# The opening of a fused triangle-and-gate kernel: first shift ahead of the second power, held-back centres, statistics whose lead grows over 33 steps

## The chip, the cores and the metric

The kernel runs on one core of one Trainium2 chip. The metric is device time in microseconds (us) of one execution. A core has five engines that run their own instruction streams in order and meet only at semaphores: TensorE (PE; its weight loads are shown as PEld), VectorE (DVE), ScalarE (ACT), GpSimd (POOL), and SyncE (SP), which here issues nearly all DMA transfers.

## The reference

Two layers on a 384 x 384 x 128 array, in float32. Only the first half of layer 0 is touched by the change:

```
z     = layernorm(x)                                 # over 128 channels
left  = (z @ Wl + bl) * sigmoid(z @ Wlg + blg)
right = (z @ Wr + br) * sigmoid(z @ Wrg + brg)
core  = einsum('bikh,bjkh->bijh', left, right)
x     = x + sigmoid(x @ Wg + bg) * (layernorm(core) @ Wout + bout)
```

Layer 1 is a gated row operation: `left * sum(right) * gate`, a projection, a residual and a layer norm. In this data the norm weights are one and the biases zero, but the kernel does not rely on it.

## The kernel before

The kernel has three stages. Stage 1 (up to about 1032 us) computes `left` and `right` and stores them to DRAM as `lr_d`. Stage 2 does the einsum, one channel at a time. Stage 3 does the output projection and all of layer 1. Every instruction is recorded with `seq`, so each engine executes its instructions exactly in the order in which the code issues them.

**Chunks, steps, halves.** Stage 1 works on 144 chunks of 8 rows of 128 tokens. A chunk is two *steps* of 4 rows, a step is two *halves* of 2 rows; 288 steps in all. For a half, `back` issues two matmuls of a 128 x 128 column tile with the 128 x 512 weights `wz` (L367; each leaves two records in the trace), two sigmoids on ACT (L377, tile `sg`, five buffers), and two products on DVE (L379, into `lr`). The PSUM tile `pr` has three buffers.

**Layer norm.** The norm's scale is applied after the matmul: `rs` is the scale of the sigmoid (L377) and a scalar of the product (L379). The mean is taken off before it. The work on a chunk's statistics runs ahead of its matmuls:

- `stats` (L264): one DVE instruction a row, from the row load `xt` (five buffers) into `st`. For the first eight chunks (PLAIN) the rows lie in the large tile `stage`.
- `powers` (L276 to L280): five small DVE operations for a *batch* of chunks, giving the variance in `nd` and parts of the mean in `mv`. `mv` has one buffer, `nd` two (for chunks from 8 on).
- `power` (L287): the power -0.5 on POOL, 8 columns at a time, into `rs`. A batch whose last power is issued joins the list `means`.
- `centres` (L297, L298, and L300 for the first eight chunks): small DVE operations that turn `nd` into the mean, with `rs` as an input.
- `store_nd` (L342 to L345), for chunks from 8 on: PE transposes `nd`, ACT copies it to `ndt` (one buffer), SP stores it to DRAM as `nd_d`. It is called at the end of step 2b - 9 for a batch that begins with chunk b (2b - 7 for chunks 8 to 11).
- `load_shift` (L140): SP loads a row of `nd_d` into `bc`, six steps before its step.
- `shift` (L312, or L315 and L316): POOL takes the mean off. For the first eight chunks it works on the rows in `stage`, which PE then transposes and ACT copies (`front`, L327 and L328). From chunk 8 on it works on the columns `xc`, loaded already transposed (L135).

**Order in a step of the main loop** (k counts steps): first up to two powers while k is at most 40, then one; then POOL's shifts, two steps ahead; then for each half `back`, after the first half `centres` and the next step's `front`, then possibly `powers` of a waiting batch, then `stats`; at the end of the step `store_nd`, the loads of columns, shift rows and row chunks, and one slice of 1 MB of finished `lr` (L353). At step 4, four shifts are done ahead, and then POOL loads another code library (L447, the code exchange), which the broadcast of L315 needs; no POOL work goes on meanwhile. At the end of step 20 `late_weights` (L228 to L235) prepares weights of the later stages on DVE, with `m2` as its own tile; at the end of step 21 PE uses `m2` in `late_products` (L241).

**The lead.** At step k the statistics run up to step k + min(25, 7 + k): two steps of statistics are done in each step until k = 18, then one. Batches are of 1 chunk for chunks 0 to 9, of 2 for chunks 10 to 17, then of 4. `powers` of a waiting batch are issued once its statistics are done and both `means` and `pows` are empty. Row chunk n (11 to 25) is asked for at step n - 7 and needs the buffer of chunk n - 5.

Of the kernel before, what the change touches and what calls it, by code (L numbers as in the profile page):

```python
# [8 lines left out]
F32 = mybir.dt.float32  # L9
# [5 lines left out]
P = 128  # L15
# [4 lines left out]
def triangle_then_gated_row_kernel(ctx: ExitStack, tc: tile.TileContext, a: dict, out: bass.AP):  # L20
# [15 lines left out]
    NG8, C = x_nat.shape[1], x_tok.shape[2]  # L36
# [6 lines left out]
    XR = 8  # L43
# [12 lines left out]
    def seq(ins):  # L56

        return tc.keep_in_program_order(ins)
# [4 lines left out]
    def load(dst, src, queue=nc.sync):  # L63
        seq(queue.dma_start(out=dst, in_=src))
# [12 lines left out]
    chunks = [(kb, ig, c) for kb in range(NB) for ig in range(NG) for c in range(G // XR)]  # L77
    kept = {(NB - 1, ig): None for ig in range(NG - KEEP, NG)}
    end2 = ctx.enter_context(ExitStack())
    with ExitStack() as ctx2:  # L80
# [16 lines left out]
        with tc.tile_pool(name="p1w", bufs=5, side="right") as wp, \  # L97
# [7 lines left out]
            NQ = XR // 4  # L105
            AHEAD, LEAD = 6, 25
# [2 lines left out]
            loaded, normed = {}, {}  # L109
            lr, full = {}, []  # L110
            batches, at = [(n, n + 1) for n in range(PLAIN)], PLAIN
            for size in [1, 1, 2, 2, 2, 2] + [4] * len(chunks):
                if at < len(chunks):
                    batches.append((at, min(at + size, len(chunks))))
                    at = batches[-1][1]
            batch = {n: b for b in batches for n in range(*b)}
            terms, pows = {}, []
# [105 lines left out]
            def late_weights():  # L223

                m2 = wp.tile([P, C], F32, tag="m2", name="m2", bufs=1)
                seq(nc.vector.tensor_scalar(m2, avg, go, -0.5, ALU.mult, ALU.mult))  # L228

                seq(nc.vector.tensor_add(wleft, wleft, weq))
                seq(nc.vector.tensor_add(bleft, bleft, beq))

                seq(nc.vector.tensor_scalar(lns, lns, -1.0, None, ALU.mult))  # L235
                return m2
# [29 lines left out]
            def powers(own, lo, hi):  # L266

                if lo == 0:
                    g = XR * (own[1] - own[0])
                    terms[own] += [sp.tile(s, F32, tag=t, name=t, bufs=c)[:, :g] for t, s, c in  # L270
                                   (("mv", [P, 4 * XR, 2], 1),
                                    ("nd", [P, 4 * XR], 2) if own[0] >= PLAIN else ("nd0", [P, XR], PLAIN),
                                    ("rs", [P, 4 * XR], 7) if own[0] >= PLAIN else ("rs0", [P, XR], PLAIN))]
                st, mv, sd, rs = (t[:, lo:hi] for t in terms[own])
                dv = st[:, :, 1]
                seq(nc.vector.tensor_add(mv, st[:, :, 1:3], st[:, :, 4:6]))  # L276
                seq(nc.vector.tensor_sub(dv, dv, st[:, :, 4]))
                seq(nc.vector.tensor_scalar(sd, mv[:, :, 1], 4.0 / C, 4.0 * EPS, ALU.mult, ALU.add))
                seq(nc.vector.tensor_mul(dv, dv, dv))
                seq(nc.vector.tensor_add(sd, sd, dv))  # L280
                pows.extend((own, c, min(c + XR, hi), (lo, hi)) for c in range(lo, hi, XR))

            def power():

                own, lo, hi, span = pows.pop(0)
                sd, rs = (t[:, lo:hi] for t in terms[own][2:])
                seq(nc.gpsimd.tensor_tensor(rs, sd, mhalf[:, :hi - lo], ALU.pow))  # L287
                if hi == span[1]:
                    means.append((own, span))
# [11 lines left out]
                    centred.add(own)  # L301

            centred = set()
            means = []

            def shift(n, q, rows=slice(0, 4)):
# [23 lines left out]
            def first_step():  # L330

                pairs = slice(0, 2), slice(2, 4)
                for s in pairs:
                    shift(0, 0, s)
                for s in pairs:
                    front(0, 0, s)

            def store_nd(own):

                g = XR * (own[1] - own[0])  # L340
                pt = tps.tile([P, 4, P], F32, tag="pt", name="pt")
                seq(nc.tensor.transpose(pt[:g, 0], nds.pop(own), ident))  # L342
                ndt = dp.tile([4 * XR, P], F32, tag="ndt", name="ndt", bufs=1)
                seq(nc.scalar.activation(ndt[:g], pt[:g, 0], AF.Copy, scale=0.5))  # L344
                seq(nc.sync.dma_start(  # L345
                    out=nd_d[own[0]:own[1]].rearrange("n (i k) -> (n i) k", k=P), in_=ndt[:g]
                ))
# [50 lines left out]
            given = 0  # L398

            def stats_to(count):  # L400

                nonlocal given
                while given < min(count, len(halves2)):
                    n, q, half = halves2[given]
                    stats(n, q, half)
                    given += 1
                    if half == 1 and q == NQ - 1:
                        ready.append(n)

            ready = []  # L410
            for k in range(AHEAD):
                for half in range(2):
                    stats_to(given + 1)
                    if k > 0 and half == 0:
                        centres(len(means))
                    if k == 1:
                        weights(half)
                if k == 0:
                    fold()
                    powers((0, 1), 0, 4)  # L420
                    power()
                elif k == 1:
                    powers((0, 1), 4, XR)
                    power()
                elif k < AHEAD - 1 and k % NQ == 1:
                    powers(batch[k // NQ], 0, XR)
                    power()
                if k == 1:
                    first_step()
                if k == 2:  # L430
                    shift(*steps[1])
            shifted = 2
# [2 lines left out]
            waiting = batches[AHEAD // NQ:]  # L435
            for k, (n, q) in enumerate(steps):
                early = len(means)
                for _ in range(min(len(pows), 1 if k > 40 else 2)):
                    power()
                early = early if k > 40 else len(means)  # L440
                more = 4 if k in (4, len(steps) - 6) else 1
                while shifted < min(len(steps), k + 2 + more):
                    shift(*steps[shifted])
                    shifted += 1
                if more > 1:
                    lib = library_config.all_libraries[10] if k == 4 else library_config.standard
                    seq(nc.gpsimd.load_library(lib))  # L447
                turned = [b for b in batches[PLAIN:] if NQ * b[0] - (TURN if b[0] >= PLAIN + 4 else TURN - 2) == k]
                for half in range(2):
                    if k == 0:  # L450

                        back(n, q, half, (lambda: front(*steps[1])) if half else None)
                    else:
                        back(n, q, half)
                        if half == 0:
                            centres(early)
                        if half == 0 and k + 1 < len(steps):
                            front(*steps[k + 1])
                    if half == 0 and not means and not pows and waiting and 2 * NQ * waiting[0][1] <= given:
                        own = waiting.pop(0)  # L460
                        powers(own, 0, XR * (own[1] - own[0]))
                    stats_to(2 * (k + min(LEAD, AHEAD + k + 1)) + half + 1)
                if q == NQ - 1:
                    del loaded[n], normed[n], columns[n]
                for b in turned:
                    assert b in centred, (k, b, waiting[:1], pows, means)
                    store_nd(b)
                if q == NQ - 1:
                    load_columns(n + 4)
                for m, mq in steps[k + FETCH:k + FETCH + 1]:  # L470
                    if m >= PLAIN:
                        load_shift(m, mq)
                for m in fetch.get(k, []):
                    load_chunk(m)
                store_slice()
                if k == 4:
                    for t, src in later:
                        load(t, src)
                if k == 20:
                    m2 = late_weights()  # L480
                if k == 21:
                    late_products(m2)
                if k == len(steps) - 2 * G // 4 + 16:
                    assert not full
                    for h in range(2):
                        load_h(h)
# [134 lines left out]
    with ExitStack() as ctx3:  # L621
# [5 lines left out]
        wp, sp, op, up = pool("p3w", 4), pool("p3s", 4), pool("p3out", 3), pool("p3u", 18)  # L627
# [215 lines left out]
        f, fetched = 0, 4 * RG  # L843
# [107 lines left out]
```

## Time and profile before

| | us |
|---|---|
| median of three runs | 3178.45 (3176.88 to 3178.5) |
| the profiled execution | 3176.98 |
| its span, first to last instruction | 3175.2 |
| first matmul of stage 2 (L580) | 1032.43 |
| PE busy over the span | 3144.1 (99%) |

PE is the engine that sets the time. In a row of an engine's timeline the columns are: start, time taken by the group, engine, line, operation, output<-inputs, shape, count, and in brackets the idle time of the engine before it with what ended it. In a row of the table of stretches the columns are: the stretch, its length, then busy time (and instructions) of PE, PEld, DVE, ACT and POOL, then the granted PE clock (1.00 is full), the busy share of the DMA engines, and GB/s. In the list of waits they are: who waited, for whom, us in all, times, the longest. A wait is put down to the link that came last, which need not be its cause.

### The profile page before, as it was taken

Reading aid. Unit: us, or ns where it says so; the run is one execution under the profiler, and the core shown is the slowest. Engines: PE = TensorE matmul, PEld = TensorE weight load, DVE = VectorE, ACT = ScalarE, POOL = GpSimd, SP = SyncE. Lnnn points to the kernel's source line nnn. Section 1 sums busy time; section 2 is a strip of 40 time slices with the busy share of each in tenths; the row PEclk is TensorE's granted clock in tenths of the full one; section 3 lists DMA queues with packets and bytes.
Section 4 is the critical chain, followed back from the end, with each engine's and each line's share of the span. In section 5 each row is a group of like instructions: output and inputs, shape, how many; then the busy total and the mean of one; then the engine's idle time right before and its main releaser. Section 6 shows DMA issues by size and latency. Waiting matters only on the chain.

```text
span 3175.2 us, 44349 instructions
## 1 busy us (share of the span) xinstructions
PE 3144.1 (99%) x11344; PEld 1875.8 (59%) x11344; DVE 2452.9 (77%) x7201; ACT 1811.9 (57%) x3793; POOL 2384.1 (75%) x3045
## 2 busy tenths in 40 slices
PE   8999999999999999999999999999999999999998
PEld 3444444444444666666666666677777777777776
DVE  8878888888875555555555788888888888888998
ACT  4444444444444333433433577777777777777776
POOL 5888888888886666666665587787788888888887
PEclk9999999999999999999999999999999999999999
DMA  4787878878782999999999865666666666666552
GB/s 157 289 326 271 329 297 308 315 288 337 272 327 86 266 283 281 285 282 282 284 282 282 302 229 211 216 225 222 218 223 218 224 217 223 219 220 219 209 209 110
DMA packets 474829, 797.41 MB, mean 251 GB/s; under 512 B 21329, under 2 KB 385297, under 8 KB 458194
## 3 DMA queue, kind: packets, MB, share of 16 engines
q1 hardware_dynamic: 473280, 792.61, 72.7%
q8 instruction: 94, 1.54, 0.2%
q10 hardware_dynamic: 1234, 1.77, 0.2%
q14 instruction: 157, 1.29, 0.1%
q0 software_dynamic: 64, 0.20, 0.0%
HBM read 508.14 MB, written 286.36 MB: 250 GB/s over the span
## 4 chain that ended last, share of the span: by engine, by line
PE 95%; POOL 2%; DVE 1%; issue 1%; DMA 1%; ACT 1%; SPq 0%; ACTq 0%; POOLq 0%; DVEq 0%
PE pr L367 28%; PE pc L580 23%; PE py L750 8%; PE pr L721 8%; PE pg L738 8%; PE pl L739 8%; PE pg L690 8%; PE py L751 4%; POOL rs L287 1%; DVE lr L379 1%; POOL xc L316 0%; DVE st L264 0%; DMA xt<-in_x_nat_dram 0%; POOL bc L315 0%; DMA stage<-in_x_nat_dram 0%
## 5 line engine op out<-in xcount | busy, mean ns | idle before, releaser
L367 PE MATMUL pr<-wz,xc 128*128 128x512 f32 x2176 | 939.9, 592 | 5.0 <-ACT sg L377 4.3
L377 ACT ACTIVATE sg<-pr,rs 128x256 f32<-128x256 f32 x1152 | 483.2, 470 | 522.3 <-ACT sg L377 346.4
L580 PE MATMUL pc<-rr,lrh 128*128 128x384 f32 x2304 | 743.3, 486 | 0.3 <-DVE lr L379 0.3
L367 PEld LDWEIGHTS pr<-wz,xc 128*128 128x128 f32 x2176 | 409.8, 190 | 522.7 <-issue 433.6
L379 DVE SCALAR_TENSOR_TENSOR lr<-pr,rs,sg 128x256 f32<-128x256 f32 x1152 | 502.3, 478 | 197.5 <-ACT sg L377 197.5
L580 PEld LDWEIGHTS pc<-rr,lrh 128*128 128x128 f32 x2304 | 452.0, 196 | 291.8 <-issue 1.1
L785 ACT ACTIVATE py<-py,nm,rs 128x128 f32<-128x128 f32 x1149 | 491.8, 429 | 158.2 <-DVE u L743 80.1
L750 PEld LDWEIGHTS py<-wo,u 128*128 128x128 f32 x2304 | 376.6, 191 | 97.5
L591 DVE TENSOR_TENSOR csum<-csum,ct 128x1152 f32<-128x1152 f32 x127 | 176.2, 1387 | 333.8 <-ACT ct L589 333.8
L750 PE MATMUL py<-wo,u 128*128 128x128 f32 x2304 | 402.1, 275 | 0.0
L589 ACT COPY ct<-pc 128x1152 f32<-128x1152 f32 x127 | 142.2, 1119 | 445.2 <-PE pc L580 439.7
L712 POOL TENSOR_TENSOR cs<-ct,rt 128x384 f32<-128x384 f32 x380 | 378.8, 998 | 7.6 <-PE pr L721 4.1
L820 POOL TENSOR_TENSOR yt<-yt,lnb 128x384 f32<-128x384 f32 x380 | 379.7, 1001 | 2.9 <-DVE yt L814 2.6
L316 POOL TENSOR_TENSOR xc<-xc,bc 128x512 f32<-128x512 f32 x272 | 345.2, 1269 | 23.9
L287 POOL TENSOR_TENSOR rs<-nd,mhalf 128x8 f32<-128x8 f32 (+1 forms) x145 | 235.7, 1628 | 157.4 <-ACT ndt L344 107.3
L765 DVE BATCH_NORM_STATS2 st<-py 128x6 f32<-128x128 f32 x1152 | 266.4, 287 | 88.9 <-PE py L751 86.9
L561 POOL COPY rr<-lrh 128x768 f32<-128x768 f32 x128 | 193.7, 1513 | 165.3 <-DMA lrh<-lr_d 154.3
L751 PE MATMUL py<-ident,x1T 128*128 128x128 f32 x1152 | 314.0, 273 | 0.0
L721 PE MATMUL pr<-cs,wc 128*128 128x384 f32 x768 | 313.5, 490 | 0.0
L738 PE MATMUL pg<-x1T,mat_L_conv_W_gate 128*128 128x384 f32 x768 | 310.7, 486 | 0.9 <-ACT g L741 0.9
L690 PE MATMUL pg<-xt,mat_L_conv_Wg 128*128 128x384 f32 x768 | 310.7, 487 | 0.3 <-ACT ct L604 0.2
L739 PE MATMUL pl<-x1T,mat_L_conv_W_left 128*128 128x384 f32 x768 | 310.5, 486 | 0.0
(125 smaller groups left out, 4284.6 us busy)
## 6 DMA issues: line engine op xcount, KB each, us to landing
lr_d<-lr SPq DMA_DIRECT2D x128, 1024.0 KB
lrh<-lr_d SPq DMA_DIRECT2D x128, 640.0 KB
xt<-in_x_row_dram SPq DMA_DIRECT2D x96, 768.0 KB
ct<-core_d SPq DMA_DIRECT2D x95, 768.0 KB
rt<-rstd_d SPq DMA_DIRECT2D x95, 768.0 KB
out_dram<-yt SPq DMA_DIRECT2D x94, 768.0 KB
core_d<-ct SPq DMA_DIRECT2D x125, 576.0 KB
xt<-in_x_nat_dram SPq DMA_DIRECT2D x136, 512.0 KB
```

The lines of the kernel that those rows point to most:

```text
L367: seq(nc.tensor.matmul(pr[:, r, :], lhsT=columns[n][:, 4 * q + 2 * half + r, :], rhs=wz, start=True, stop=True))
L377: seq(nc.scalar.activation(sg[r], pr[:, r, 2 * H:], AF.Sigmoid, scale=rs[r]))
L379: seq(nc.vector.scalar_tensor_tensor(t[:, :, c * XR + r0 + r, :], pr[:, r, :2 * H].rearrange("k (h s) -> k h s", s=2), rs[r], sg[r].rearra ...
L580: seq(nc.tensor.matmul(banks[ib], lhsT=t[:, kb, ib * P:(ib + 1) * P, 0], rhs=rr[:, kb], start=(kb == 0), stop=(kb == NB - 1),))
L690: seq(nc.tensor.matmul(pg[:, :N], lhsT=wg0, rhs=r["xT"], start=True, stop=True))
L721: seq(nc.tensor.matmul(pr[:, :N], lhsT=wc, rhs=r["cs"], start=True, stop=True))
L738: seq(nc.tensor.matmul(pg2[:, :N], lhsT=wgate, rhs=r["x1T"], start=True, stop=True))
L739: seq(nc.tensor.matmul(pl[:, :N], lhsT=wleft, rhs=r["x1T"], start=True, stop=True))
L750: seq(nc.tensor.matmul(py[:, s], lhsT=r["u"][:, s], rhs=r["wo"], start=True, stop=False))
L751: seq(nc.tensor.matmul(py[:, s], lhsT=r["x1T"][:, s], rhs=ident, start=False, stop=True, is_transpose=True))
L785: seq(nc.scalar.activation(py[:, s], py[:, s], AF.Identity, bias=bias, scale=scale))
L820: seq(engine.tensor_tensor(yt, yt, lnbb, ALU.add))
```

## The change

1. In the opening, `first_step` (POOL's two subtracts of step 0, PE's transposes, ACT's copies) is issued ahead of the second power rather than after it.
2. In the main loop one power at most is issued in a step. The number of centres to issue is none at steps 5 and 6, the number of batches waiting *before* this step's power at steps after 6, and the number after it at steps up to 4.
3. The lead grows by one a step up to step 11 (to 18), then by one every three steps, and reaches 25 at step 32. Batches of 2 run to chunk 23 (there are seven), and batches of 4 follow from 24 to the end.
4. `mv` has its own tag for each size of batch, with three buffers for one chunk, two for two, one for four. `free` lets the powers of a batch start while fewer batches of its size than that are in flight.
5. `m2` is no longer a tile of its own: it takes the one buffer of `ndt`, which is enlarged to 128 partitions.

The numbers of instructions hardly change: PE has one `nd` transpose more, ACT one copy more, SP one store more. In the order of SP's queue only the stores of `nd` move.

```diff
-            for size in [1, 1, 2, 2, 2, 2] + [4] * len(chunks):
+            for size in [1, 1] + [2] * 7 + [4] * len(chunks):
...
-                m2 = wp.tile([P, C], F32, tag="m2", name="m2", bufs=1)
+                m2 = dp.tile([P, C], F32, tag="ndt", name="m2", bufs=1)
...
-                                   (("mv", [P, 4 * XR, 2], 1),
+                                   ((f"mv{g}", [P, g, 2], {XR: 3, 2 * XR: 2}.get(g, 1)),
...
+            def free(own):
+                flying = {p[0] for p in pows} | {p[0] for p in means}
+                size = own[1] - own[0]
+                return sum(o[1] - o[0] == size for o in flying) < {1: 3, 2: 2}.get(size, 1)
...
-                ndt = dp.tile([4 * XR, P], F32, tag="ndt", name="ndt", bufs=1)
+                ndt = dp.tile([P, P], F32, tag="ndt", name="ndt", bufs=1)
...
                     powers((0, 1), 4, XR)
+                    first_step()
                     power()
                 elif k < AHEAD - 1 and k % NQ == 1:
                     powers(batch[k // NQ], 0, XR)
                     power()
-                if k == 1:
-                    first_step()
...
-                for _ in range(min(len(pows), 1 if k > 40 else 2)):
+                for _ in range(min(len(pows), 1)):
                     power()
-                early = early if k > 40 else len(means)
+                early = 0 if k in (5, 6) else early if k > 6 else len(means)
...
-                    if half == 0 and not means and not pows and waiting and 2 * NQ * waiting[0][1] <= given:
+                    if half == 0 and waiting and 2 * NQ * waiting[0][1] <= given and free(waiting[0]):
...
-                    stats_to(2 * (k + min(LEAD, AHEAD + k + 1)) + half + 1)
+                    stats_to(2 * (k + min(LEAD, AHEAD + min(k + 1, 12 + (k - 11) // 3))) + half + 1)
```

## The prediction

> **What bounds the kernel now.** I read the page first, then a table of engine busy time over stretches of the opening, then what TensorE (PE) waited for, then the timelines of single engines around each wait.
>
> ```profile
> span 3175.2 us, 44349 instructions
> PE 3144.1 (99%) x11344; PEld 1875.8 (59%) x11344; DVE 2452.9 (77%) x7201; ACT 1811.9 (57%) x3793; POOL 2384.1 (75%) x3045
> ```
>
> ```profile
> 0.00:25.00 25.00, 19.14 (x49) 9.17 (x50) 18.33 (x89) 6.78 (x15) 12.73 (x20) 0.93 0.78 281
> 25.00:50.00 25.00, 20.02 (x64) 9.57 (x63) 21.30 (x94) 11.16 (x26) 12.45 (x10) 1.00 0.12 39
> 50.00:75.00 25.00, 23.83 (x72) 10.50 (x70) 24.18 (x94) 13.09 (x32) 14.20 (x11) 1.00 0.46 161
> 75.00:100.00 25.00, 22.57 (x58) 9.59 (x58) 24.28 (x93) 11.40 (x28) 19.66 (x18) 1.00 0.62 215
> 100.00:150.00 50.00, 48.06 (x122) 21.26 (x121) 38.85 (x135) 22.86 (x57) 39.92 (x35) 1.00 0.76 295
> 150.00:200.00 50.00, 48.44 (x115) 21.20 (x114) 37.55 (x124) 23.77 (x59) 36.77 (x34) 1.00 0.85 317
> 200.00:300.00 100.00, 100.00 (x236) 43.85 (x235) 80.96 (x255) 48.82 (x120) 83.47 (x74) 1.00 0.84 324
> ```
>
> The second number of a row is PE's busy time. From 200 us on PE is never idle in this stage, and the change moves nothing in later stages. Before 200 us the idle time is 5.9 + 5.0 + 1.2 + 2.4 + 1.9 + 1.6 = 17.9 us. That is all the change can win, 0.56% of the time, and part of it lies before the first data are there. Losses have no such bound.
>
> ```profile
> PE pr L367 <- ACT sg L377: 10.4, 8, 2.9
> PE pt L327 <- POOL stage L312: 5.3, 4, 3.5
> ```
>
> From PE's timeline, the waits once step 2's tile is there (20.80 us) are 2.07 (at 40.74), 2.91 (47.75), 0.18, 0.30, 0.58, 0.33, 0.58, 0.56, 0.34, 0.63 (the last at 95.21), 0.38 (114.23), 1.56 (143.89) and 1.56 (173.26): 11.98 us. ACT is only the last link: behind it is VectorE (DVE), which executes in order and stands in front of GpSimd (POOL).
>
> ```profile
> 40.74 1.96 PE L367 MATMUL pr<-wz,stage 128*128 128x512 f32 x4 [2.07 <-ACT sg L377]
> 47.75 1.96 PE L367 MATMUL pr<-wz,stage 128*128 128x512 f32 x4 [2.91 <-ACT sg L377]
> ```
> ```profile
> 35.98 0.96 DVE L298 TENSOR_TENSOR nd<-mv,nd 128x8 f32<-128x8 f32 x1
> 44.39 0.17 DVE L297 TENSOR_TENSOR nd<-nd,rs 128x8 f32<-128x8 f32 x1 [2.63 <-POOL rs L287]
> 108.00 0.87 DVE L228 TENSOR_SCALAR m<-avg,col_L_conv_onorm_g 128x128 f32<-128x128 f32 x1
> 141.69 0.65 DVE L297 TENSOR_TENSOR nd<-nd,rs 128x32 f32<-128x32 f32 x1 [2.68 <-POOL rs L287]
> ```
>
> A centre operation (L297, L298) takes 0.17 alone and 0.96 when a GpSimd subtract runs beside it; where its power is not done it waits, and the products `lr` queued behind it wait too.
>
> **The change, part by part.**
>
> *First shift ahead of the second power.* PE's and ACT's order stay. On POOL two half subtracts (0.60 each) go ahead of a power of 1.02. They start when L300 ends (7.38) and end at 8.6; the second power's input comes at 9.24, so that power is not delayed. PE's first transposes come 2.9 us earlier, but PE then waits for step 2's subtract, which waits for DVE and POOL. There the gain is smaller: the centres from 10.37 to 11.54 took 1.17 us beside those subtracts; without them the same three take 0.40 (15.46 to 15.86). So 0.77 us; bounds 0 and 2.9.
>
> *Centres held back.* At steps 5 and 6 none is issued, so DVE no longer meets the 2.63 us wait behind the code exchange (GpSimd idle from 37.9 to 42.67), and PE's 2.91 and 0.18 go. What is late next: six held centre operations at 0.20 come together at step 7, 1.2 us, of which I let 1.1 reach PE (up to 3 if a subtract runs beside them). The wait at 40.74 stays: step 4's centres still stand beside four subtracts. Gain 2.0; bounds 0 and 3.1.
>
> *One power a step, and a slower lead.* Up to step 11 the lead is the same; from 12 to 32 DVE does 5.3 statistics a step for 8, 0.5 us less at 0.195 each, where it was 24.28 of 25 us busy. A subtract follows each power where two powers (3.24) stood before it. The seven waits from 66 to 95 us, 3.3 us, should go; bounds 1 and 3.3. With the count of centres taken ahead of this step's power at every step after 6, DVE no longer stands in front of a power issued in the same step: 0.38 + 1.56 + 1.56 go, 3.5; bounds 2 and 3.5. Sum of gains: 0.8 + 2.0 + 3.3 + 3.5 = 9.6 us.
>
> *m2 in ndt's buffer.* This is the cost that the few words of the change do not show. That pool tag has one buffer. m2 (L228, end of step 20) must wait until the store of batch (14, 15)'s `ndt`, issued at step 19, has left it. That store is on SP's queue behind the load of chunk 25, put there at step 18. This load needs the buffer that chunk 20's statistics free, and with the slower lead the last of those are the statistics of step 20 itself, directly ahead of m2. So DVE stops for a whole round through the queue: one load of 0.5 MB, one `lr_d` store of 1 MB, then the small store. An estimate from the rows: 2.5 us fixed (the first load was issued at 0.73 and used at 3.87, with 0.6 of it transfer) and 1.57 MB at 413 GB/s, 3.8 us: 6.3. Queued behind m2 on DVE are products and statistics; PE needs m2 at L241, which it reached 1.1 us after DVE reached L228 (109.13 against 108.00), and 0.5 pass from m2 to the matmul. Loss 6.3 + 0.5 - 1.1 = 5.7. Bounds: 1 (a small transfer in an empty queue, with part of it covered) and 8 (the 2 KB row issued at 121.04 reached POOL at 127.03, 6.0, and two issues of 1.0 ahead of it).
>
> ```profile
> 121.04 1.69 SPq L140 DMA_DIRECT2D bc<-nd_d  x2
> 127.03 0.79 POOL L315 PARTITION_BROADCAST bc<-bc  x1 [2.27 <-DMA bc<-nd_d]
> ```
>
> ```profile
> 12.60:16.00 3.40, 3.40 (x6) 0.50 1.03 413
> ```
>
> *Half clock.* This row of the table of stretches (PE alone) shows PE's granted clock at 0.50 for 3.4 us soon after PE had stood still for 3.45 us (7.5 to 10.97). There it cost little, for PE waited at 20.80 anyway. A stop of 5.7 us in mid-stage should bring such a stretch with nothing to cover it: 1.6 us; bounds 0 and 1.7. PE's wait for step 2 grows to 1.2 + 2.9 - 0.8 = 3.3 us, nearly as long as that stop; I count half, 0.8 (0 to 1.7). [...]
>
> *Smaller batches, freer powers.* One more `ndt` transpose, 0.1 us. But `nd` keeps two buffers. The powers of (22, 23) come in the first half of step 26 (96 half steps are then given), while (18, 19) leaves its buffer only with the transpose at the end of step 27. DVE stands until PE has done three more halves, and then needs five small operations (0.5), six statistics (1.2) and two products (0.8), plus 0.2 to hand over, before PE goes on: 2.7 us; bounds 0 and 5.2 (three halves of 1.72).
>
> Sum of losses: 5.7 + 1.6 + 0.8 + 2.7 + 0.1 = 10.9 us. Net +1.3. The profiled run took 3176.98 us (span 3175.2 and 1.8 around it), which gives 3178.3; the median of the three runs lies 1.5 higher, which gives 3179.8. I take 3179 between them.
>
> **The rivals.**
>
> *Faster.* The m2 wait does not reach PE (the store is out when DVE arrives, or DVE runs later than I think). It takes 5.7 + 1.6 with it: 3171.7. For it: gains and this loss are of one size, so the sign hangs on it, and in the run before the store was issued 4.6 us ahead of m2 (103.41). Against it: the load in front of the store cannot start before DVE's own last statistics.
>
> *Slower.* SP's queue runs dry of row loads. Chunks 21 to 28 are asked for up to two steps before their buffer is free, and behind them on SP's queue stand the columns and the shift rows. A row is asked for six steps ahead and used by POOL some four steps later, 13.8 us; two steps of wait (6.9) and a queue of 6.0 leave 0.9. From 1 us more a load on, POOL and then PE wait; over eight loads that is 8 us: 3187. Against it: nothing of this kind showed beyond POOL's 2.27 at 127.03, which PE did not feel.
>
> *The DVE-bound waits stay.* If the statistics are not what makes DVE last, most of the 3.3 and half of the 3.5 remain: 3179 + 5 = 3184.
>
> **How the numbers follow.** Net near zero 0.60, faster rival 0.20, slower rival 0.12, waits that stay 0.08. 0.2% is 6.4 us, about what a measurement of this kernel can tell from no change; the bounds are 3172.1 and 3184.8. The likeliest case alone spans 3174 to 3184; taking in the faster rival and most of the slower ones the range is 3171.3 to 3186. Faster 0.20, within 0.62, slower 0.18.
>
> **What would show it.** Right: PE's first transposes near 8.0 us and step 2's near 20.0; no DVE wait for a power between 40 and 50; one PE stop of 5 to 6 us ahead of L241 near 106 us, with L228 waiting for the store of `ndt`, and a row of half clock after it; a PE wait of 2 to 3 us about six steps later, with L278 standing for the `ndt` transpose; no waits like those at 143.89 and 173.26. Wrong: no stop at L241; or POOL waiting for `bc` rows and PE for `xc` between 80 and 150 us; or `lr` still waited for through 66 to 95 us.

## The result, and the profile after

The changed kernel takes 3183.58 us (median of 22 runs, 3180.96 to 3187.39). The kernel before takes 3177.89 on the same chip (22 runs, 3176.55 to 3179.6). The ratio is 1.0018, 95% interval 1.0011 to 1.0025: a loss of 5.7 us that is just inside the 0.2% called "within" in the prediction. The prediction of 3179.0 had the sign, and its range of 3171.3 to 3186 holds the time. The runs also spread more than before: over 6.4 us, where the kernel before spreads over 3.1. Ratios leave out runs that were disturbed; there was one, 5591.69 us in `late_loads` below.

The profiled execution has a span of 3180.1 us, against 3175.2. In the changed kernel the line numbers of stage 1 behind `free` are six higher: L373 is L367 of the kernel before, L350 is L344, L333 is L327, and L322 is L316. The table of stretches of the changed kernel, columns as before:

```profile
0.00:25.00 25.00, 18.64 (x46) 9.13 (x47) 17.43 (x88) 6.86 (x14) 13.61 (x20) 0.93 0.78 279
25.00:50.00 25.00, 22.93 (x72) 11.20 (x71) 23.97 (x101) 12.99 (x30) 13.21 (x10) 1.00 0.16 50
50.00:75.00 25.00, 24.42 (x77) 11.47 (x76) 22.90 (x98) 13.35 (x34) 16.20 (x13) 1.00 0.47 169
75.00:100.00 25.00, 25.00 (x64) 11.02 (x62) 21.20 (x84) 12.48 (x31) 18.76 (x16) 1.00 0.72 241
100.00:150.00 50.00, 37.06 (x88) 17.06 (x87) 31.84 (x118) 16.32 (x40) 30.40 (x27) 0.86 0.68 256
150.00:200.00 50.00, 50.00 (x120) 21.88 (x119) 40.85 (x134) 24.65 (x61) 41.10 (x36) 1.00 0.83 320
```

Everything that the change was to mend is mended: between 25 and 100 us and from 150 us on PE is idle for 2.65 us, where it was idle for 10.1 before. All of that, and more, is lost in the one row from 100 to 150, which has 12.9 us of idle PE and a mean clock of 0.86. On PE's timeline the first row below is step 2's tile, and the four others hold all the stops after it:

```profile
19.73 1.12 PE L333 MATMUL pt<-ident,stage 128*128 128x128 f32 x4 [4.55 <-POOL stage L318]
41.12 1.95 PE L373 MATMUL pr<-wz,stage 128*128 128x512 f32 x4 [2.07 <-ACT sg L383]
53.53 1.95 PE L373 MATMUL pr<-wz,stage 128*128 128x512 f32 x4 [0.56 <-ACT sg L383]
112.15 0.80 PE L241 MATMUL pw<-mat_L_conv_Wout,m 128*128 128x128 f32 x2 [10.21 <-DVE m L228]
140.07 14.01 PE L373 MATMUL pr<-wz,xc 128*128 128x512 f32 x32 [2.72 <-ACT sg L383]
```

The stop ahead of L241 is the wait for `m2`. The timelines of ACT, SP, DVE and POOL in the same kernel show how it comes about:

```profile
95.77 0.25 ACT L350 ACTIVATE ndt<-pt 16x128 f32<-16x128 f32 x1
101.80 0.47 DVE L264 BATCH_NORM_STATS2 st<-xt 128x6 f32<-128x128 f32 x2
102.30 0.34 SPq L128 DMA_DIRECT2D xt<-in_x_nat_dram  x1
102.69 0.42 SPq L359 DMA_DIRECT2D lr_d<-lr  x1
103.21 0.38 SPq L351 DMA_DIRECT2D nd_d<-ndt  x1
110.73 1.37 DVE L228 TENSOR_SCALAR m<-avg,col_L_conv_onorm_g 128x128 f32<-128x128 f32 x1 [8.45 <-DMA xc<-in_x_tok_dram]
110.75 1.26 POOL L322 TENSOR_TENSOR xc<-xc,bc 128x512 f32<-128x512 f32 x1
```

`ndt` is ready at 96.0, but SP, which works in order, issues its store only at 103.21: the load ahead of it waits for the buffer that the statistics at 101.80 free. The store then takes 7.5 us more. DVE waits for it from 102.28 to 110.73. (The row names a load that came last by the profile; the runs below show that it is the store.) L228 then takes 1.37 us, beside a subtract that starts on POOL at 110.75; in the runs below, without such a neighbour, it takes 0.27 to 0.32.

The clock in that stop, in stretches of 2 us of PE alone (columns: stretch, length, PE busy, clock, DMA share, GB/s):

```profile
102.00:104.00 2.00, 0.00 (x0) 1.00 0.94 339
104.00:106.00 2.00, 0.00 (x0) 0.66 0.92 289
106.00:108.00 2.00, 0.00 (x0) 0.50 1.00 416
112.00:114.00 2.00, 1.85 (x9) 0.50 0.11 45
114.00:116.00 2.00, 2.00 (x5) 0.50 0.00 0
116.00:118.00 2.00, 2.00 (x4) 0.50 0.00 0
118.00:120.00 2.00, 2.00 (x6) 0.93 0.02 4
```

The clock falls to half 2.7 us into the stop (104.64, from the share 0.66) and comes back at 118.28, 6.1 us after work has begun again. At full clock those 6.1 us of work would have taken about half as long: the four records of L373 at 41.12 above took 1.95 us at 1.00, and the same four at 43.31 in `m2_in_avg_nd3` (below) took 3.62 at 0.50. So about 3.1 us are lost on top of the 10.21. The stop in the opening is followed by another half-clock stretch, from 19.30 to 22.70, of which 3.0 us are work: 1.5 lost.

**An account of stage 1.** The first matmul of stage 2 comes at 1037.06, for 1032.43 before: 4.63 us later, of the 4.9 us that the spans differ by. The account splits that time in four: the start of step 2's transposes, all of PE's stops after it, half of the time that PE worked at half clock after it (from the clock in stretches of 1 us), and the rest.

| profiled execution | step 2's tile | stops after it | half clock | rest | stage 2 begins |
|---|---|---|---|---|---|
| before | 20.80 | 11.98 | 0 | 999.65 | 1032.43 |
| after | 19.73 | 15.56 | 4.56 | 997.21 | 1037.06 |
| after less before | -1.07 | +3.58 | +4.56 | -2.44 | +4.63 |

The rest is nearly a constant. It is 2.4 lower after, where thirteen stops have become four: by that estimate a stop costs 0.2 to 0.3 more than the idle time shown, which no run tests by itself. The loss of this change is thus not its stops alone, but as much the half clock behind them.

### The profile page after: what moved, and what is told of

It is laid out like the page before. It is cut to its first block, busy times and chain, and to the rows that moved or that the text cites. A ratio compares the mean times of both kernels' runs of the same rounds, so it can differ in the third digit from the quotient of the medians.

```text
span 3180.1 us, 44362 instructions
## 1 busy us (share of the span) xinstructions
PE 3144.7 (99%) x11345; PEld 1878.7 (59%) x11345; DVE 2459.8 (77%) x7208; ACT 1811.9 (57%) x3794; POOL 2402.9 (76%) x3045
## 4 chain that ended last, share of the span: by engine, by line
PE 97%; DVE 2%; DMA 1%; ACT 0%; POOL 0%; issue 0%; SPq 0%; DVEq 0%; POOLq 0%; ACTq 0%
PE pr L373 30%; PE pc L585 23%; PE py L755 8%; PE pr L726 8%; PE pg L743 8%; PE pl L744 8%; PE pg L695 8%; PE py L756 4%; DVE st L264 0%; DVE lr L385 0%; DMA core_d<-ct 0%; DMA xc<-in_x_tok_dram 0%; POOL rs L287 0%; PE pq L703 0%; PE pt L348 0%
## 5 line engine op out<-in xcount | busy, mean ns | idle before, releaser
L373 PE MATMUL pr<-wz,xc 128*128 128x512 f32 x2176 | 940.5, 593 | 2.7 <-ACT sg L383 2.7
L373 PEld LDWEIGHTS pr<-wz,xc 128*128 128x128 f32 x2176 | 411.0, 190 | 519.5 <-issue 432.9
L322 POOL TENSOR_TENSOR xc<-xc,bc 128x512 f32<-128x512 f32 x272 | 345.2, 1269 | 24.0
```

The costliest lines, as they stand in the source:

```text
L373: seq(nc.tensor.matmul(pr[:, r, :], lhsT=columns[n][:, 4 * q + 2 * half + r, :], rhs=wz, start=True, stop=True))
```

## The experiments

Every run is compared with the kernel before on its own chip (medians 3177.0 to 3178.0). "Theory" in the first expectations is the prediction's mechanism with the sizes of the result: the stop for `m2`, and the half clock behind it, make the loss. One execution of each version was profiled, and it is not always a typical one: those of `m2_in_avg_nd3`, `store_on_act` and `nd3_warm` took 1.6 to 2.9 us more than their medians.

### Is it the buffer that m2 shares with ndt?

`m2_in_avg` is the changed kernel with `m2` written over its own input `avg`, which nothing reads later.

```diff
-                m2 = dp.tile([P, C], F32, tag="ndt", name="m2", bufs=1)
+                m2 = avg
```

> The changed kernel, but m2 is written in place over avg, which nothing reads afterwards, so it waits for no store. Theory (m2 waits for ndt's store): the stop of 10.2 us ahead of L241 shrinks to under 1 us and the half clock from 104.6 to 118.3 us goes (6.1 us of work at half speed, 3.1 us): 13 us less than the changed kernel, about 3170, which is 7 to 8 us below the kernel before. The wait of 2.7 us at L278 stays. Rival A (the backlog of loads and lr_d stores would stop the steps there in any case, m2 only meets it first): another wait of 5 us or more appears between 100 and 125 us, on bc or xc, and the time stays above 3177. Rival B (the slower lead is what costs): no gain beyond 2 us.

Measured: 3173.87 us (3172.64 to 3175.47), ratio 0.9987 [0.9978, 0.9996]. Against 1.0018 that is 9.9 us won by this one line. The stop ahead of L241 is down to 0.64. So without the shared buffer the change wins 4 us. It misses the expected 3170: by the account 4.2 us are lost to other half-clock stretches, nearly as much as after (4.56). One follows the next stop of the same profile (PE's timeline, then PE's row in a stretch):

```profile
103.95 0.49 PE L241 MATMUL pw<-mat_L_conv_Wout,avg 128*128 128x128 f32 x2 [0.64 <-DVE avg L228]
129.81 15.97 PE L373 MATMUL pr<-wz,xc 128*128 128x512 f32 x32 [2.88 <-DVE st L264]
```
```profile
131.00:134.00 3.00, 3.00 (x5) 0.50 0.79 251
```

`before_m2_shared` does the reverse: the kernel before, with only the sharing.

```diff
-                m2 = wp.tile([P, C], F32, tag="m2", name="m2", bufs=1)
+                m2 = dp.tile([P, C], F32, tag="ndt", name="m2", bufs=1)
...
-                ndt = dp.tile([4 * XR, P], F32, tag="ndt", name="ndt", bufs=1)
+                ndt = dp.tile([P, P], F32, tag="ndt", name="ndt", bufs=1)
```

> The kernel before with one part of the change alone: m2 takes the buffer of ndt. Theory: the store of ndt was issued at 103.41 there, 4.6 us ahead of m2 at 108.0, since no load held it back; with some 7 us through the queue m2 waits 2 to 4 us and PE 1 to 3, too short for a half clock: 3179 to 3181. If sharing alone carried the whole loss: 3188 or more (a stop of 10 us and half clock after it). If it costs only with the slower lead: 3177.9 unchanged.

Measured: 3182.89 us (3179.53 to 3187.38), ratio 1.0016 [1.0007, 1.0025]. The sharing alone costs 5.0 us, nearly as much as the whole change, and brings the wide spread with it. DVE's and PE's timelines:

```profile
111.50 0.29 DVE L228 TENSOR_SCALAR m<-avg,col_L_conv_onorm_g 128x128 f32<-128x128 f32 x1 [3.07 <-DMA nd_d<-ndt]
```
```profile
111.84 0.49 PE L241 MATMUL pw<-mat_L_conv_Wout,m 128*128 128x128 f32 x2 [2.21 <-DVE m L228]
```

The store is issued at about the same time as after (103.74 for 103.21), and is out at about the same time too (111.5 for 110.7). But DVE comes to L228 at 108.4 here and at 102.3 after, and PE to L241 at 109.6 and at 101.9, so the stop is 2.2 us for 10.2. L241 starts no sooner after (112.15) than here (111.84): what the change wins ahead of that point it gives back in the stop. By the account this profile has two half-clock stretches after step 2 (41.58 to 44.98 and, behind the stop of 2.21 us, 113.26 to 116.66, 3.4 us lost), and its stops, 12.27 us in all, are hardly longer than before's.

### What makes the store late?

`late_loads`: row chunks 21 to 25 are asked for two steps later (26 one step, later ones as before), so that the load of chunk 25 stands behind the store.

```diff
-                fetch.setdefault(max(2 + (n - PLAIN) // 2, n - 7, 2 * n - LEAD - 7), []).append(n)
+                fetch.setdefault(max(2 + (n - PLAIN) // 2, n - (7 if n < 21 else 5), 2 * n - LEAD - 7), []).append(n)
```

> The changed kernel with m2 still in ndt's buffer, but row chunks 21 to 27 are asked for two steps later, when their buffers are free, so the store of ndt does not stand behind a load that waits for the statistics of step 20. Theory: the store goes out when ndt is written, about 97 to 99 us instead of 103.2, and is out when DVE reaches m2 or 1 to 4 us later: PE's stop at L241 under 4 us, no or little half clock, 3170 to 3175. Rival A (a small store needs 7 to 8 us behind stores and loads whatever is ahead of it): stop of 4 to 6 us, 3176 to 3180. Rival C (the order on SP does not matter): 3183 unchanged.

Measured: 3177.11 us, ratio 0.9994 [0.9985, 1.0003], at the edge between the two expectations. Of the 9.9 us that the sharing costs, 6 to 8 are won back: the stop ahead of L241 is 3.23. SP's, DVE's and PE's timelines:

```profile
96.55 0.32 SPq L351 DMA_DIRECT2D nd_d<-ndt  x1
98.81 0.36 SPq L128 DMA_DIRECT2D xt<-in_x_nat_dram  x1
```
```profile
105.32 0.29 DVE L228 TENSOR_SCALAR m<-avg,col_L_conv_onorm_g 128x128 f32<-128x128 f32 x1 [2.54 <-DMA nd_d<-ndt]
```
```profile
105.66 0.80 PE L241 MATMUL pw<-mat_L_conv_Wout,m 128*128 128x128 f32 x2 [3.23 <-DVE m L228]
```

The store is issued as soon as `ndt` is there, 6.7 us earlier than after, and still needs 8.8 us to leave the buffer. The load directly ahead of it explains the late issue, not the slow passage.

`store_on_act` gives the store another queue.

```diff
-                seq(nc.sync.dma_start(
+                seq(nc.scalar.dma_start(
                     out=nd_d[own[0]:own[1]].rearrange("n (i k) -> (n i) k", k=P), in_=ndt[:g]
```

> The changed kernel (3183.6) with m2 still in ndt's buffer, and one line different: the store of ndt is issued on ACT's own queue in place of SP's. Theory A (the store is slow because it stands in SP's queue behind the bytes of loads and slices issued before it, and not because it comes late): on an empty queue it takes some 2.5 us from its issue near 103, VectorE waits until about 106 for 110.7, the stop ahead of L241 falls from 10.2 to about 5 us and with it one or two of the four stretches of half clock (1.7 us each): 3175 to 3178. Theory B (the engines that move the data are shared and full, whatever the queue): the store is out near 110.5 all the same, 3183.6.

Measured: 3174.58 us (3173.3 to 3177.41), ratio 0.9994 [0.9985, 1.0002]; 7.6 us faster than after by the ratios, so theory B falls. ACT's and DVE's timelines:

```profile
98.25 0.25 ACT L350 ACTIVATE ndt<-pt 16x128 f32<-16x128 f32 x1
98.54 0.31 ACTq L351 DMA_DIRECT2D nd_d<-ndt  x1
104.68 0.32 DVE L228 TENSOR_SCALAR m<-avg,col_L_conv_onorm_g 128x128 f32<-128x128 f32 x1
```

DVE does not wait at all, though `m2` still has `ndt`'s buffer. Theory A was right in direction and missed one part: the store is not issued near 103 but at 98.54, since it no longer stands behind SP's waiting load. Its packets on ACT's queue run from 101 to 103 us, while the DMA engines are full (shares of 1.06 and 1.03 in those two us): 4.5 us from the issue, for 7.5 and 8.8 on SP's queue. So most of the delay belongs to SP's queue: an issue held up by 7.2 us (96.02 to 103.21) in the changed kernel, and a slower passage. That the bytes of earlier transfers on the same queue make it slower is the author's guess, which no run shows by itself.

`m2_step21`: the changed kernel with `late_weights` at step 21 and `late_products` at step 22.

```diff
-                if k == 20:
-                    m2 = late_weights()
                 if k == 21:
+                    m2 = late_weights()
+                if k == 22:
```

> The changed kernel (3183.6) with m2 still in ndt's buffer, and the late weights and products one step later (21 and 22 for 20 and 21). Theory (VectorE comes to L228 before the store has left the buffer; only the difference counts): VectorE comes 3.4 us later (two halves of 1.72), the store leaves at the same time, so the stop ahead of L241 is 10.2 - 3.4 = 6.8 us, and at least one of the four stretches of half clock goes with it: 3177.5 to 3180. Rival (the stop is a round through SP's queue that starts with VectorE's own last statistics and moves along with it, as the prediction had it): the stop stays near 10 us and the time near 3183.6.

Measured: 3181.46 us (3178.47 to 3182.88), ratio 1.0012 [1.0004, 1.0021], above the expected range. The stop itself falls by 4.9 us, more than expected, so the rival is out. DVE's and PE's timelines, and PE's row for the time behind the stop:

```profile
111.99 0.29 DVE L228 TENSOR_SCALAR m<-avg,col_L_conv_onorm_g 128x128 f32<-128x128 f32 x1 [6.18 <-DMA nd_d<-ndt]
```
```profile
112.33 0.80 PE L241 MATMUL pw<-mat_L_conv_Wout,m 128*128 128x128 f32 x2 [5.33 <-DVE m L228]
```
```profile
112.40:120.40 8.00, 8.00 (x17) 0.50 0.65 238
```

But after a stop of half the length PE works 8.3 us at half clock, where it was 6.1 after the long one, and the stops of the opening and at the end of step 27 have longer half-clock work behind them as well: 8.4 us are lost to it by the account, for 4.6. That goes with a gain of only about 2 us for a stop 4.9 us shorter; the intervals of this version and of after overlap.

### The buffers of nd

`m2_in_avg_nd3` is `m2_in_avg` with a third buffer.

```diff
-                                    ("nd", [P, 4 * XR], 2) if own[0] >= PLAIN else ("nd0", [P, XR], PLAIN),
+                                    ("nd", [P, 4 * XR], 3) if own[0] >= PLAIN else ("nd0", [P, XR], PLAIN),
```

> The same with a third buffer for nd. Theory: the powers of (22, 23) no longer wait for the transpose at the end of step 27, the PE wait of 2.7 us about six steps after L241 goes, time 2 to 3 us below the kernel with m2 in avg, about 3167. Rival: the wait passes to the next batch or to ndt, and nothing is won (within 1 us).

Measured: 3169.69 us (3167.99 to 3172.62), ratio 0.9975 [0.9966, 0.9984]; every one of its runs is faster than every one of `m2_in_avg`. The stop of 2.88 goes, and with it the half-clock stretch behind it (1.7 us): 4.2 us in the medians, nearly their sum. DVE's timeline in the changed kernel shows the wait behind that stop, for the transpose that frees `nd` (L348); with the third buffer L278 does not wait:

```profile
137.38 0.17 DVE L278 TENSOR_SCALAR nd<-mv 128x16 f32<-128x16 f32 x1 [2.30 <-PE pt L348]
```

This version is 8 us faster than the kernel before.

### The parts of the change, undone one at a time

The base is `m2_in_avg_nd3` (0.9975), in which neither new stop hides anything. The intervals of all the versions in this part and the next overlap with the base's, so differences of 2 to 3 us are read together with the stops in the profiles.

`nd3_old_opening`: `first_step` stands behind the second power again.

```diff
                     powers((0, 1), 4, XR)
-                    first_step()
                     power()
...
+                if k == 1:
+                    first_step()
```

> The change with m2 written over avg and three nd buffers (median 3169.7, 0.9975 of before), and one part undone: the first step's shift and transposes stand behind the second power again. Theory: the new opening brings step 2's tile 1.07 us earlier (19.73 for 20.80), but turns one wait of 3.45 us in the opening and one of 1.2 us ahead of step 2 into one stop of 4.5 us ahead of step 2, and one or two stretches of half clock of 3.41 us then fall on work that nothing covers (1.5 to 2.9 us). So undoing it gains 0.5 to 1.8 us: 3168 to 3169.2, ratio 0.9969 to 0.9973, and no half clock after 20.8 us. Rival (the prediction's sum, 0.8 won and 0.8 lost): no difference, 3169.7. Second rival (the half clock is made up for later, at the wait of 2.07 us near 41 us): undoing it costs the 1.07 us, 3170.8.

Measured: 3169.28 us (3167.57 to 3170.1), ratio 0.9972 [0.996, 0.9983]: no difference that can be told from none, as by the prediction's sum. In the profiles step 2's tile comes 0.6 us later than in the base, and the 3.0 us lost to half clock behind it are gone; but the medians do not show the 0.5 to 1.8 us that were expected for that. The base's profiled execution took 2.9 us more than its median, so its half clock need not be what the other runs have.

`nd3_old_centres`: the old count of centres.

```diff
-                early = 0 if k in (5, 6) else early if k > 6 else len(means)
+                early = early if k > 40 else len(means)
```

> The same base (3169.7) with the old count of centres: up to step 40 those behind this step's own power are taken too, and steps 5 and 6 hold none back. Theory: DVE stands again behind the power that waits for the code exchange (2.9 and 0.2 us at PE near 48 us, for which 0.8 us at step 7 goes), and behind the power of the same step later on (0.4 + 1.6 + 1.6 in the kernel before): 5 to 6 us slower, 3174.7 to 3175.7, ratio 0.9990 to 0.9994. Rival: with one power a step the later waits stay away by themselves, and only the one near 48 us comes back: 2.0 to 2.5 us slower, 3171.7 to 3172.2.

Measured: 3173.29 us (3170.65 to 3175.32), ratio 0.9984 [0.9976, 0.9993]: 2.9 us slower, nearer to the rival. One stop comes back on PE's timeline, the one behind the code exchange; those after 100 us do not:

```profile
50.38 3.48 PE L373 MATMUL pr<-wz,stage 128*128 128x512 f32 x4 [2.88 <-ACT sg L383]
```

`nd3_two_powers`: up to two powers a step until step 40.

```diff
-                for _ in range(min(len(pows), 1)):
+                for _ in range(min(len(pows), 1 if k > 40 else 2)):
```

> The same base (3169.7) with up to two powers a step again up to step 40 (the count of centres ahead of the powers stays, and so does the slower lead). Theory (the prediction's, which gave the pair of parts 3.3 us, most of it to the statistics): 0 to 1.5 us slower, 3169.7 to 3171.2. Rival: the second power of 1.64 us ahead of a subtract was the cause of the waits from 66 to 95 us; then 2 to 3.3 us slower, 3171.7 to 3173.0, and PE waits for pr, lr or xc in that stretch.

Measured: 3172.07 us (3171.04 to 3173.42), ratio 0.9981 [0.9972, 0.999]: 1.9 us slower by the ratios. PE's timeline shows where:

```profile
120.25 7.13 PE L373 MATMUL pr<-wz,xc 128*128 128x512 f32 x16 [1.50 <-POOL xc L322]
157.54 14.00 PE L373 MATMUL pr<-wz,xc 128*128 128x512 f32 x32 [1.52 <-POOL xc L322]
```

These are stops of the size of the two of 1.56 before, and they wait for POOL's subtract, which stands behind two powers in a row. POOL's timeline in this kernel ahead of the second stop:

```profile
152.09 3.24 POOL L287 TENSOR_TENSOR rs<-nd,mhalf 128x8 f32<-128x8 f32 x2
156.20 1.29 POOL L322 TENSOR_TENSOR xc<-xc,bc 128x512 f32<-128x512 f32 x1
```

and in the kernel before, ahead of its stop that ends at 143.89, with PE's weight load (PEld) for the matmul behind it:

```profile
138.42 3.24 POOL L287 TENSOR_TENSOR rs<-nd,mhalf 128x8 f32<-128x8 f32 x2
142.53 1.27 POOL L316 TENSOR_TENSOR xc<-xc,bc 128x512 f32<-128x512 f32 x1
143.86 0.30 PEld L367 LDWEIGHTS pr<-wz,xc 128*128 128x128 f32 x2 [2.36 <-POOL xc L316]
```

In both PE goes on within 0.1 us of that subtract's end. In the kernel before a sigmoid that stands behind the late centre ends at 143.85, 0.05 after the subtract (143.80), which is why the list of waits names ACT there: both chains end together, so earlier centres alone could hardly have won that stop. The rival had the cause, but not the place: from 66 to 95 us PE stays busy but for 0.06 us.

`nd3_old_lead`: the lead of before.

```diff
-                    stats_to(2 * (k + min(LEAD, AHEAD + min(k + 1, 12 + (k - 11) // 3))) + half + 1)
+                    stats_to(2 * (k + min(LEAD, AHEAD + k + 1)) + half + 1)
```

> The same base (3169.7) with the old lead, which grows by one step a step up to 25. Theory (the prediction's): eight statistics a step for 5.3 make VectorE the last again between 66 and 95 us; the seven waits there come back in good part, and the kernel is 1 to 3.3 us slower: 3170.7 to 3173.0, ratio 0.9978 to 0.9985. Rival: those waits came from two powers standing in a row in GpSimd's queue; then the lead alone brings nothing back, 3169.7, and two powers a step do.

Measured: 3168.21 us (3167.93 to 3169.18), ratio 0.9969 [0.9958, 0.9981]: not slower, if anything faster. The table of stretches of this kernel:

```profile
66.00:95.00 29.00, 28.04 (x77) 12.46 (x76) 28.46 (x113) 14.41 (x36) 23.69 (x20) 1.00 0.69 248
```

and of the base:

```profile
66.00:95.00 29.00, 29.00 (x82) 13.29 (x81) 24.85 (x100) 15.16 (x38) 21.21 (x18) 1.00 0.56 202
```

VectorE is as full as the prediction said (28.46 of 29 us), and PE is idle for under 1 us. It does not show in the time: this run has no stop ahead of L241 and no such stops as the base's 0.81 and 0.43 near 118 and 129 us.

### Is the half clock in the opening worth anything?

`nd3_warm` is the base with four matmuls more in the stop of 4.55 us; their result is overwritten by the transposes. `nd3_lead_warm` is the same on `nd3_old_lead`.

```diff
                     pt = tps.tile([P, 4, P], F32, tag="pt", name="pt")
+                    for _ in range(4 if (n, q) == steps[2] else 0):
+                        seq(nc.tensor.matmul(pt, lhsT=avg, rhs=avg.unsqueeze(1).to_broadcast([P, 4, P]), start=True, stop=True))
                     for r in range(s.start, s.stop):
```

> The change with m2 over avg and three nd buffers (3169.7), and four matmuls more of 128x512, 0.85 us each, whose result is overwritten, in PE's stop of 4.55 us ahead of step 2's transposes. Theory: one or two stretches of half clock of 3.41 us (near 19.6 to 26.4 us) go and nothing else changes, 1.5 to 2.9 us: 3166.8 to 3168.2, ratio 0.9965 to 0.9970. Rival: that loss is made up for at the wait of 2.07 us near 41 us, which is then as much longer; 3169.7.

> The same four matmuls together with the old lead (25 steps reached by one step a step; without the matmuls 3168.2, ratio 0.9969). Theory: the same 1.5 to 2.9 us less: 3165.3 to 3166.7, ratio 0.9960 to 0.9965, and no half clock left in the opening. Rival: 3168.2. This is the version that would beat both kernels by most.

Measured: `nd3_warm` 3167.36 us (3165.99 to 3168.96), ratio 0.9969 [0.9958, 0.9981]; `nd3_lead_warm` 3166.29 us (3165.68 to 3168.82), ratio 0.9967 [0.9955, 0.9979]. PE's timeline of `nd3_warm`:

```profile
15.37 3.60 PE L333 MATMUL pt<-avg 128*128 128x512 f32 x8
20.07 0.66 PE L335 MATMUL pt<-ident,stage 128*128 128x128 f32 x4 [1.11 <-POOL stage L318]
```

PE's row for the same stretch in `nd3_warm`:

```profile
16.00:28.00 12.00, 10.89 (x33) 1.00 0.57 172
```

and in the base:

```profile
16.00:28.00 12.00, 7.55 (x17) 0.72 0.54 159
```

In neither run is there a half clock anywhere in the first 200 us. `nd3_warm` is 1.9 us faster than its base by the ratios, as expected, though the intervals overlap. `nd3_lead_warm` gains less on its own base, `nd3_old_lead`, than was expected (0.6 by the ratios), well inside the intervals; in the opening the profile of `nd3_old_lead` had one half-clock stretch to lose, that of `m2_in_avg_nd3` had two. So the matmuls take the half clock away, and what that is worth in time is not settled. `nd3_lead_warm` has the lowest median here, 10.7 us faster than the kernel before on its chip.

By the account of stage 1, the rest is 997.2 to 999.7 us in all of the fourteen profiles, and 999.1 at most in the twelve without the many small stops: step 2's tile, the stops and the half clock explain the length of stage 1 within about 2.5 us.

## Why the prediction was right, point by point

**First shift ahead of the second power** (0.8 won). The tile came 1.07 us earlier, so the size was right. PE's stop ahead of it was 4.55 us and not 3.3, and the half clock behind it cost 1.5 in the profile for the 0.8 counted. In sum nothing much, and undoing it gave no difference that can be told from none.

**Centres held back** (2.0). Right: 2.91 and 0.18 gone, 0.56 given back for 1.1, the wait near 41 us unchanged at 2.07. Undoing the count costs 2.9.

**One power a step, and a slower lead** (3.3, seven waits). All seven went, but the lead, which the working gave as the reason, is not it: with the old lead alone most of them stay away. Two of the seven (66.38 and 69.44) could not have come from it at all, since they lie ahead of step 12 on VectorE (its first product is at 73.5), and up to step 11 the lead is the same. The working's 5.3 statistics a step for 8 also holds only up to step 18; from 19 to 32 it is 5.3 for 4. Two powers a step alone do not bring them back either, nor does the old count of centres. Which mixture of the parts made them, the smaller batches and freer powers included, was not settled.

**Centres counted ahead of the power** (3.5, with both waits of 1.56). The time was won, but this step named the wrong part. With the old count no such stop comes back; with two powers a step stops of 1.50 and 1.52 do, and they wait for POOL, which in the kernel before ended together with the chain over the centre. Those microseconds belong to the single power a step.

**m2 in ndt's buffer** (5.7). The mechanism was right and the term mis-sized: 10.21, above its bound of 8. Of the 4.5 us of difference, 2.15 lie in VectorE's wait (8.45 for 6.3): SP issued the store 0.9 us after VectorE's arrival, and the passage took 7.5, in which the queue moved at only 279, 250 and 328 GB/s between 103 and 106 us for the 413 reckoned with. Another 0.9 is the pass to PE (1.42 for 0.5, with L228 beside a subtract), and 1.4 is the lead: PE came to L241 0.34 us ahead of VectorE, not 1.1 behind it. That lead was read off the kernel before, whose VectorE was late; the change itself made VectorE early.

**Half clock after that stop** (1.6, bounds 0 and 1.7). This bound failed too. It allowed one stretch of 3.4 us; the work at half clock was 6.1 us, 3.1 lost.

**nd's two buffers** (2.7). The stop was 2.72, to the digit. A third buffer was worth 4.2, since in other executions a half-clock stretch follows that stop as well.

So the sum of +1.3 became +4.6 in the profiles and +5.7 in the medians through two sizes, the stop for `m2` (+4.5) and the half clock (4.56 for 2.4, +2.2), against gains that came out 3.3 us larger in the profile, mostly in what many small stops seem to cost beyond their shown idle time. That the time stayed in the range was partly luck: losses 6.7 us too small and gains 3.3 us too small cancelled in part, and 6.8 us of the gains were put down to the lead and to the count of centres, which, undone alone, bring back 1.0 us of those stops or none. The faster rival was what `m2_in_avg` made: 3173.87 for 3171.7. Of the slower rival nothing showed before the stop: POOL's wait for a row (2.37, at 109.88) came while PE was standing anyway.

## What to carry to other kernels

A buffer shared with a tile that a DMA reads put that DMA's queue into the path of the tile's next writer: VectorE waited 8.45 us here. SP issued in order, so a load that waited for a buffer held up the small store behind it by 7.2 us. Such a wait grew by what the rest of the change won ahead of it (PE's stop was 2.21 us with the sharing alone and 10.21 with the whole change), so size it against the schedule after, not before. A stop of PE is to be priced with the half clock behind it: after every unfilled stop of 3.2 us or more in stage 1, 3.0 to 8.3 us of work ran at half clock here, and half of that is lost. Matmuls that do nothing, in a stop that cannot be avoided, took the half clock away (a mean clock of 1.00 for 0.72 from 16 to 28 us).

## What the runs showed of the hardware

**Half clock comes in pieces of one length.** Every stretch of half clock in the first 200 us of the fourteen profiles is 3.40 to 3.42 us long or two, three or four times that (6.82 to 6.84, 10.24, 13.66). After stops of one length, 4.53 to 4.55 us in the opening, one piece followed in four profiles and two in five. So the same stop lost 1.5 to 1.8 us in the first four and 2.5 to 3.0 in the others. That one kernel differs like this from run to run, and that its spread comes from it, was not tested: each has one profile.

**A stop much shorter than a piece can suffice.** In `m2_in_avg_nd3` a half clock from 43.46 to 46.88 follows a stop of 2.08 us; the same stop in `m2_in_avg` (2.07, at 42.49) is followed by none, and neither is one of 2.91 us in the kernel before. PE's timeline of the first, and its row:

```profile
43.31 3.62 PE L373 MATMUL pr<-wz,stage 128*128 128x512 f32 x4 [2.08 <-ACT sg L383]
```
```profile
43.60:46.80 3.20, 3.20 (x5) 0.50 0.00 0
```

The stops of 2.21 us in `before_m2_shared`, which had been expected to be too short for it, and of 2.88 in `m2_in_avg` were each followed by a whole piece as well (113.26 to 116.66 and 130.92 to 134.34).
